# Two-expert tiles first, early masked adds, one select for two heads, and a new order of the end stage

## The chip, the cores and the metric

The kernel runs on one core of one Trainium2 chip. The metric is the time of one execution in microseconds on that core. A core has a matrix engine (PE, whose weight loads are listed as PEld), a vector engine (DVE), a scalar engine (ACT), a general engine (POOL) and a queue engine (SP) that here issues most DMA transfers. Each engine works through its own instructions in order and waits on semaphores for the others.

## The reference

The input is a query of 2048 rows by 512 columns (`T`, `E`), in float32. After a layer norm two things are computed from the same rows and added to the input:

```
xn = layernorm(x)
q1, q2, k1, k2, v = projections of xn, 16 heads, rotary on q and k
a1, a2 = causal softmax attention of (q1, k1) and (q2, k2) over v
f = rfft(a1) - lambda * rfft(a2), along the rows, times a fixed low pass
attn = rms norm(irfft(f)) @ Wout
ffn = sum over the 2 best of 8 experts of  w * (silu(xn @ w1) * (xn @ w3)) @ w2
      + (silu(xn @ sw1) * (xn @ sw3)) @ sw2
out = x + attn + ffn
```

An expert has an inner width of 352, the shared expert (`sw`) one of 704.

## The kernel before

**The stages.** Up to about 255 us of the profile the kernel does the layer norm, the gate, the projections and the first tiles of the shared expert. Then comes `middle`, up to about 1241 us: the attention, with the experts' work laid between its pieces. `ending` closes the program: the low pass, the RMS norm, the product with `Wout`, and the sum of all parts.

**The attention stream.** `middle` cuts the attention into 32 chunks, one for each pair of heads `g` (8) and each block of 512 queries `qc` (4, the last block first). A chunk is a list of units. For a unit, `scores` makes up to two products of queries and keys in PSUM (L822), ACT takes their exponential into `pt` (L835), and where the keys lie on the diagonal ("masked" units) POOL zeroes what lies above it with `affine_select` (L840). Later `values` multiplies `pt` with the values `vd` (L862), and `added` sums it on DVE for the softmax's denominator (L876 for a chunk's first, L879). When a chunk has ended, `sums` and `finish` turn its outputs and sums on PE (L888, L900, L901), DVE takes the reciprocal `rcp` (L903) and the normalised `o_n` (L908), and `put` writes it to `vd`. When all four chunks of a pair of heads are through, `folded` prepares their rows for the low pass in eight steps on POOL (on DVE for the last pair, L966 being one of its last lines). A masked unit comes in three kinds: the whole diagonal tile `d`; tiles `d+1` and `d+3` together; and tile `d+2` of both heads together (`last` in `units`).

**The loop.** The 544 units go by fours, 136 iterations of some 7 us. In each one the scores of two units come first, then the values of the units before, then the other two scores. On DVE follow the adds of units held back, the unmasked ones of the first two units, the experts' steps with the other unmasked adds between them, and at last all masked adds of the four units:

```
added(before)
added(u for u in units[:2] if not masked(u))
later = [u for u in units[2:] if not masked(u)]
while True:
    work()
    added(later[:1])
```

The engines keep the order in which the program issues (`manual_schedule`), so this text is the order on DVE. After the adds come the steps of `folded`: none if a unit of this iteration is masked, one if a unit of the next is, otherwise two.

**The experts.** `experts` is a generator; each `yield` gives its cost, and `work` calls it as often as keeps pace with the stream. It does the shared expert's tiles up to about 595 us and then 34 routed tiles of 128 rows (`NR`). The first 28 (`NP`) belong to one expert each. The other six hold 64 rows of one expert and 64 of another, and so need two experts' weights. `rows_of` gathers a tile's rows on POOL, `transposed` turns them (`xT`), `up_first` and `up_third` are the products `xh` and `xg` (L180) with a tanh between, `turned_back` turns the result into `uT` (L206 on PE, L208 and L209 on DVE), and `down` is the product `xy` (L216), which ACT scales (L225) and SP stores to `ys` (L228).

**The weights.** There are two places in SBUF, each with `wu` (1408 KB) and `wd` (768 KB). `fetch_up` (L146) and `fetch_down` (L149) load one place. Behind the second product of a tile, the `wu` places that it used are filled with what comes two halves later, and behind its down product the `wd` places:

```
for n in sets[j]:
    m = n + 2 - len(halves)
    es.append(routed(halves[n + 2]) if m < 0 else wex[NX + m : NX + m + 1])
    fetch_up(es[n + 2], n % 2, nc.sync)
```

A one-expert tile so uses one place, while the other is loading for the next tile. A two-expert tile uses both. Behind the last tiles the shared expert's weights are loaded (`wex[NX]`, `wex[NX + 1]`) for the last rows of it, which the end stage does (`wh`, L246; `ws`, L256 on ACT and L257 on DVE). SP also loads the queries `qS` (L739, eight transfers) and keys `kS` (L727) for coming chunks.

**The end.** `ending` first does the shared expert's last `wh` and `ws`, and the low pass: products of `vd` and `fold` with the table `conv` (L1141) and sums on DVE (L1186 to L1205). Meanwhile `fetched` loads the rows of the input into `res` and adds the shared expert's rows (`ysh`) and twice the routed rows (`ys`, indirect, L1125) by accumulating DMAs on POOL, 12 tiles ahead; `still` goes on with the rest. Then, for each of eight pairs of row tiles: `prepared` (`y` on DVE, its square on ACT), `means` and `scales` (root on ACT, L1227, Newton steps and `a`, L1234, on DVE), `across` (turn on PE, L1262, copy on ACT, L1264), `projected` (`po`, L1270) and `finished` (`res` plus `po`, L1275, and the store). `last` does the last tile in two halves (L1284 to L1287). Buffers come from the pools `tail1` and `tail`; `ws`, `diff` and `first` lie in `tail` with the rest. `stored(y, ysh[NT - 1], 0.5)` writes the last shared tile from DVE.

Of the kernel before, what the change touches and what calls it, by code (L numbers as in the profile page):

```python
# [47 lines left out]
NP = (T * TOP // HALF - NX) // 2  # L48
WUP = NE * 2 * FI
# [18 lines left out]
def block_kernel(  # L68
# [527 lines left out]
    def middle(general):  # L596


        with ExitStack() as pools:
# [29 lines left out]
            def experts():  # L629
# [7 lines left out]
                for t0 in range(EARLY, NT - 1, TQ):  # L637
# [3 lines left out]
                    for n, us in enumerate(chunks(xnT[:, :, cols], u_last)):  # L641
# [7 lines left out]
                        elif last and n == 3:  # L649
                            ps = bank([P, 2, NR], "ps_w")  # L650
                            for i in range(2):
                                nc.tensor.transpose(ps[:, i, :], who_sb[:, 0, :, i], ident[:NR, :NR])
                            nc.vector.tensor_copy(tok, ps[:, 0, :])
                            nc.vector.tensor_copy(wcol, ps[:, 1, :])
                        elif last and n == 5:


                            xr = [rows_of(0), rows_of(1)]
                            es = [routed(0)]
                            fetch_up(es[0], 0, nc.sync)  # L660
                        yield 3.45 * (t1 - t0) / TQ
                    if last:
                        es.append(routed(2))
# [13 lines left out]

                sets = [[j] if j < NP else [2 * j - NP, 2 * j - NP + 1] for j in range(NR)]
                halves = [2 * j + i for j in range(NR) for i in range(len(sets[j]))]
# [4 lines left out]
                def tile_down(j, uT):  # L684
                    return places(j, 1), uT, ys[j * P : (j + 1) * P, :], wcol[:, j : j + 1]

                for j in range(NR):
# [5 lines left out]
                    if j + 2 < NR:  # L693
                        xr.append(rows_of(j + 2))
# [93 lines left out]

            class Chunk:
# [21 lines left out]
                def scores(self, unit):  # L811
# [24 lines left out]
                    for _, kb, _, col, _ in unit:  # L836
                        if kb >= qc * TQ and not general:

                            part = pt[:, :, col : col + P]
                            nc.gpsimd.affine_select(  # L840
                                out=part, in_=part, pattern=[[0, 2], [1, P]], compare_op=ALU.is_ge, fill=0.0,
                                base=0, channel_multiplier=-1,
# [174 lines left out]
            def masked(entry):  # L1017
                _, c, unit = entry
                return any(kb >= c.qc * TQ for _, kb, *_ in unit)

# [8 lines left out]
            for i in range(0, len(stream), 4):  # L1029
# [22 lines left out]
                added(u for u in units[:2] if not masked(u))  # L1052
                later = [u for u in units[2:] if not masked(u)]
# [7 lines left out]
                added(u for u in units if masked(u))  # L1061
                if any(map(masked, units)) or not shared:
                    steps = 0
                else:
                    steps = 1 if any(map(masked, stream[i + 4 : i + 8])) else 2
# [25 lines left out]
    def ending():  # L1091
# [3 lines left out]
        with tc.tile_pool(name="tail1", bufs=1) as t1, tc.tile_pool(name="tail", bufs=2) as tp, tc.tile_pool(  # L1095
            name="tail_ps", bufs=4, space=PSUM
        ) as fps, tc.tile_pool(name="conv_ps", bufs=2, space=PSUM) as zps, tc.manual_schedule(
# [5 lines left out]
            _, _, _, _, (_, _, stored), _ = expert(tp, fps)  # L1103
            hidden, gated, times, _, result = shared_expert(tp, fps, 2)
# [47 lines left out]
            def copied(z):  # L1152
                diff = tp.tile([P, 2, E], F32, tag="diff", name="diff")
# [29 lines left out]
            first = tp.tile([P, E], F32, tag="first", name="first", bufs=1)  # L1183
# [128 lines left out]
            for n in range(NT // 2):  # L1312
# [4 lines left out]
                if n == 1:  # L1317
                    stored(y, ysh[NT - 1], 0.5)
                if n + 1 < NT // 2:
# [3 lines left out]
                if ahead is not None:  # L1323
                    finished(2 * n - 1, ahead)
                    still(2 * n - 1)
                if n + 2 < NT // 2:
                    pairs[n + 2].means()
                if n + 1 < NT // 2:
                    now, po = po, projected(after)
                    finished(2 * n, now)  # L1330
                    still(2 * n)
            finished(NT - 2, po)
# [137 lines left out]
```

## Time and profile before

| | |
|---|---|
| runs | 1361.46, 1357.98, 1360.07 us; median 1360.07 |
| profiled execution | 1360.14 us |
| its span, first to last instruction | 1358.3 us |
| mean granted clock of PE | 0.994 |
| busy: PE, DVE, ACT, POOL | 1312.6, 1005.4, 688.4, 626.3 us |
| stages, PE idle in them: 255 to 716 us | 1.3 us of 461 |
| 716 to 1183 us | 10.6 us of 467 |
| 1183 to 1241 us | 7.6 us of 58 |
| 1241 us to the end | 14.3 us of 117 |

The span is what lies between the first and the last instruction. An engine's busy time is the sum of its instructions; a wait in brackets in a timeline row is the idle time ahead of it on its own engine, with what ended it. `x8` in a row means eight instructions of one kind run together. The windows view gives, for each stretch, the busy time of PE, PEld, DVE, ACT and POOL with the number of instructions, then the granted clock of PE, the share of the DMA engines and GB/s. The waits view gives in one line the total, the number of times and the longest.

### The profile page before, as it was taken

How to read it: one execution, taken by the hardware profiler on the slowest of the kernel's cores; microseconds unless marked ns; L12 is line 12 of the kernel's file. 1: busy time of each engine (PE TensorE's matmuls, PEld its weight loads, DVE VectorE, ACT ScalarE, POOL GpSimd, SP SyncE). 2: the span in 40 equal slices, each digit the busy share in tenths (PEclk: the TensorE clock that was granted, in tenths of full speed). 3: DMA queues.
4: the chain of work that ended last, by engine and by line, in shares of the span. 5: the costliest groups of instructions: out<-in, count | busy, mean ns of one | idle time of the engine just before them, and what ended most of it. 6: DMA issues, size and time to landing. Idle time of an engine off the chain costs nothing.

```text
span 1358.3 us, 20810 instructions
## 1 busy us (share of the span) xinstructions
PE 1312.6 (97%) x7554; PEld 600.3 (44%) x7554; DVE 1005.4 (74%) x1344; ACT 688.4 (51%) x847; POOL 626.3 (46%) x671
## 2 busy tenths in 40 slices
PE   7999999999999999999999999899999999987998
PEld 3444444334443444445444444344544444443544
DVE  7049883287668778868889986778898788764785
ACT  2311110265656566676666666566676666640221
POOL 0002330012221323235968984778589469421764
PEclk9999999999999999999999999999999999998999
DMA  9406673200211122235665656555565666777997
GB/s 375 171 16 171 201 196 97 89 15 32 75 43 31 40 75 82 74 123 170 190 194 143 226 176 180 181 173 174 185 194 178 210 189 230 262 294 293 175 219 169
DMA packets 75578, 214.29 MB, mean 158 GB/s; under 512 B 12244, under 2 KB 12696, under 8 KB 69576
## 3 DMA queue, kind: packets, MB, share of 16 engines
q1 hardware_dynamic: 62744, 185.68, 41.7%
q0 software_dynamic: 11056, 22.78, 8.6%
q10 hardware_dynamic: 1664, 4.38, 0.9%
q8 instruction: 63, 1.03, 0.3%
q14 instruction: 51, 0.42, 0.1%
HBM read 169.69 MB, written 43.10 MB: 157 GB/s over the span
## 4 chain that ended last, share of the span: by engine, by line
PE 65%; DVE 6%; POOL 5%; DMA 3%; issue 1%; ACT 1%; SPq 0%; DVEq 0%; ACTq 0%; POOLq 0%
PE ps_o L862 16%; PE ps_s L822 12%; PE wh L246 8%; PE xy L216 6%; PE xg L180 5%; PE xh L180 5%; PE wy L284 4%; PE ps_sum L888 2%; DMA wu<-in_wex_dram 2%; POOL pt L840 1%; PE po L1270 1%; DMA wd<-in_wex_dram 1%; DVE sum L879 1%; PE ps_ot L900 1%; PE ps_x L165 1%
## 5 line engine op out<-in xcount | busy, mean ns | idle before, releaser
L879 DVE TENSOR_TENSOR sum<-sum,pt 128x1024 f32<-128x1024 f32 (+3 forms) x576 | 621.4, 1128 | 36.3 <-ACT pt L835 21.6
L835 ACT ACTIVATE pt<-ps_s 128x1024 f32<-128x1024 f32 x544 | 527.3, 1023 | 184.3 <-PE ps_s L822 131.0
L840 POOL TENSOR_SCALAR_AFFINE_SELECT pt<-pt 128x256 f32<-128x256 f32 x256 | 171.0, 693 | 358.7 <-ACT pt L835 357.5
L862 PE MATMUL ps_o<-pt,vd 128*32 128x512 f32 (+3 forms) x2560 | 268.0, 534 | 4.1 <-POOL pt L840 4.1
L822 PE MATMUL ps_s<-qS,kS 64*128 64x512 f32 (+3 forms) x1280 | 203.8, 406 | 2.0 <-DVEq L1335 1.6
L822 PEld LDWEIGHTS ps_s<-qS,kS 64*128 64x128 f32 x1280 | 97.1, 185 | 177.0 <-issue 95.9
L246 PE MATMUL wh<-xnT,wu 128*128 128x512 f32 (+1 forms) x352 | 150.4, 574 | 0.0
L862 PEld LDWEIGHTS ps_o<-pt,vd 128*32 128x32 f32 x2560 | 66.9, 109 | 125.8 <-issue 103.5
L545 PE MATMUL ps_x<-xnT,wqk_sb 128*128 128x512 f32 x256 | 110.5, 593 | 0.0
L498 POOL DMA_INDIRECT who<-pairs,slot x32 | 33.1, 1034 | 165.9 <-DVE pairs L495 104.9
L216 PE MATMUL xy<-wd,uT 128*128 128x512 f32 (+3 forms) x240 | 97.1, 606 | 7.7 <-DVE rcp L903 6.3
L246 PEld LDWEIGHTS wh<-xnT,wu 128*128 128x128 f32 x352 | 64.1, 190 | 72.7 <-issue 56.5
L180 PE MATMUL xh<-wu,xT 128*128 128x352 f32 (+1 forms) x320 | 90.5, 473 | 4.2 <-DMA wu<-in_wex_dram 3.3
L917 POOL TENSOR_TENSOR vd<-o_n 128x128 f32<-128x128 f32 x60 | 62.2, 1057 | 65.6 <-DVE o_n L908 65.5
L180 PE MATMUL xg<-wu,xT 128*128 128x352 f32 (+1 forms) x320 | 88.6, 468 | 0.0
L545 PEld LDWEIGHTS ps_x<-xnT,wqk_sb 128*128 128x128 f32 x256 | 48.4, 190 | 60.6 <-issue 60.6
L284 PE MATMUL wy<-wd,ws 128*128 128x512 f32 x160 | 74.8, 603 | 0.0
L257 DVE SCALAR_TENSOR_TENSOR ws<-ws,wh 128x512 f32<-128x512 f32 (+4 forms) x26 | 16.7, 644 | 73.6 <-ACT ws L256 73.6
L1125 POOL DMA_INDIRECT res<-ys,slot x32 | 54.9, 1715 | 25.3 <-DMA res<-ysh 13.5
L562 ACT CAST hi<-turned 128x1024 fp32r<-128x1024 f32 x16 | 16.7, 1045 | 93.9 <-DVE turned L560 70.9
L180 PEld LDWEIGHTS xh<-wu,xT 128*128 128x128 f32 (+1 forms) x320 | 48.0, 176 | 31.7 <-issue 6.5
L180 PEld LDWEIGHTS xg<-wu,xT 128*128 128x128 f32 (+1 forms) x320 | 46.6, 174 | 34.4 <-issue 14.8
(254 smaller groups left out, 1416.8 us busy)
## 6 DMA issues: line engine op xcount, KB each, us to landing
wu<-in_wex_dram SPq DMA_DIRECT2D x44, 1408.0 KB
wd<-in_wex_dram SPq DMA_DIRECT2D x43, 768.0 KB
kS<-parts_k SPq DMA_DIRECT2D x128, 128.0 KB
qS<-parts_q SPq DMA_DIRECT2D x256, 64.0 KB
ys<-y_sb SPq DMA_DIRECT2D x34, 256.0 KB
parts_q<-hi SPq DMA_DIRECT2D x32, 256.0 KB
parts_k<-hi SPq DMA_DIRECT2D x16, 256.0 KB
parts_k<-turned SPq DMA_DIRECT2D x16, 256.0 KB
```

The lines of the kernel that those rows point to most:

```text
L180: nc.tensor.matmul(dst[r, :], xT[:, c, r], w[:, o : o + FI], start=(c == 0), stop=(c == NE - 1), skip_group_check=True,)
L216: nc.tensor.matmul(y[r, :], uT[:m, ic, r], w[:m, ic * E : (ic + 1) * E], start=(ic == 0), stop=(ic == NF - 1), skip_group_check=True,)
L246: nc.tensor.matmul(dst, w_sb[o // WUP][0][:, o % WUP : o % WUP + P], x[:, c, :], start=(c == 0), stop=(c == NE - 1))
L284: nc.tensor.matmul(y, us[i][:, t * P : (t + 1) * P], w_sb[i // NF][1][:, i % NF * E : (i % NF + 1) * E], start=(i == 0), stop=(i == SCH - 1),)
L545: nc.tensor.matmul(ps[:, i, :], wqk_sb[st, qk][:, i, c, :], xnT[:, c, cols], start=(c == 0), stop=(c == NE - 1),)
L822: nc.tensor.matmul(to, k, queries[2 * g + h, qc][r, off : off + w], start=True, stop=not general)
L835: nc.scalar.activation(pt[:, :, used], ps[:, :, used], AF.Exp, scale=SCALE)
L840: nc.gpsimd.affine_select(out=part, in_=part, pattern=[[0, 2], [1, P]], compare_op=ALU.is_ge, fill=0.0, base=0, channel_multiplier=-1,)
L862: nc.tensor.matmul(self.o[r : r + 32, off:], vd[:, kb, v0 : v0 + 32], pt[:, s, :], start=first, stop=self.ended, skip_group_check=True,)
L879: nc.vector.tensor_add(to, to, pt)
L917: eng.tensor_add(vd[:, self.qc * TQ : (self.qc + 1) * TQ, v0 : v0 + 32], self.o_n[:, :, h, 0, :], self.o_n[:, :, h, 1, :],)
L1125: nc.gpsimd.indirect_dma_start(out=came[k], out_offset=None, in_=ys, in_offset=bass.IndirectOffsetOnAxis(ap=slot[:, step - 2, order[k] : o ...
```

## The change

The order of routed tiles becomes `ORDER`: the six two-expert tiles, then the 28 of one expert; `sets`, `halves`, `places` and `tile_down` follow it. The masked adds of an iteration's first two units are issued with the unmasked ones, ahead of the experts' steps; those of the other two stay at the end. In a `last` unit one `affine_select` over four blocks of 128 columns takes the place of two over two. Ahead of an iteration with masked units a step of `folded` is issued only if another pair of heads is ready or the last pair is in work. In the end stage the last shared tile is scaled and stored by ACT, `ws`, `diff` and `first` come from a pool of their own (`tail2`), and `finished` of the two tiles moves: one ahead of `across` and `prepared`, the other ahead of `means`.

```diff
NR = NS - 2
 NP = (T * TOP // HALF - NX) // 2
+ORDER = [*range(NP, NR), *range(NP)]
 WUP = NE * 2 * FI
 WCOL = WUP + NF * E
 CONVS = 23
...
                         elif last and n == 5:
-                            xr = [rows_of(0), rows_of(1)]
-                            es = [routed(0)]
+                            xr = [rows_of(j) for j in ORDER[:2]]
+                            es = [routed(2 * ORDER[0])]
                             fetch_up(es[0], 0, nc.sync)
                         yield 3.45 * (t1 - t0) / TQ
                     if last:
-                        es.append(routed(2))
+                        es.append(routed(2 * ORDER[0] + 1))
                         fetch_up(es[1], 1, nc.sync)
                     for t in range(t0, t1):
                         y = result(us, t - t0, range(NF))
...
                 xT, late = transposed(xr.pop(0)), None
                 yield 0.6
-                sets = [[j] if j < NP else [2 * j - NP, 2 * j - NP + 1] for j in range(NR)]
-                halves = [2 * j + i for j in range(NR) for i in range(len(sets[j]))]
+                sets, halves = [], []
+                for tj in ORDER:
+                    n = 1 if tj < NP else 2
+                    sets.append(range(len(halves), len(halves) + n))
+                    halves += [2 * tj + i for i in range(n)]
                 def places(j, part):
                     return [w_sb[n % 2][part] for n in sets[j]]
                 def tile_down(j, uT):
-                    return places(j, 1), uT, ys[j * P : (j + 1) * P, :], wcol[:, j : j + 1]
+                    tj = ORDER[j]
+                    return places(j, 1), uT, ys[tj * P : (tj + 1) * P, :], wcol[:, tj : tj + 1]
                 for j in range(NR):
                     if j > 0:
...
                     yield 2.9 if late else 2.4
                     u = up_third(places(j, 0), xT, half)
                     if j + 2 < NR:
-                        xr.append(rows_of(j + 2))
+                        xr.append(rows_of(ORDER[j + 2]))
                     for n in sets[j]:
                         m = n + 2 - len(halves)
...
                 nc.vector.tensor_copy(shift, ps.rearrange("p t q -> p (t q)"))
                 return shift
+            def masked(chunk, unit):
+                return any(kb >= chunk.qc * TQ for _, kb, *_ in unit)
             class Chunk:
...
                     pt = pp.tile([P, 2, QC], F32, tag="pt", name="pt")
                     used = slice(min(c for *_, c, _ in unit), max(c + w for *_, c, w in unit))
                     nc.scalar.activation(pt[:, :, used], ps[:, :, used], AF.Exp, scale=SCALE)
-                    for _, kb, _, col, _ in unit:
-                        if kb >= qc * TQ and not general:
-                            part = pt[:, :, col : col + P]
+                    if masked(self, unit) and not general:
+                        cols = [col for *_, col, _ in unit]
+                        if cols == [0, 2 * P]:
+                            chosen = [pt.rearrange("p s (h q) -> p (s h) q", h=2)[:, :, :P]]
+                        else:
+                            chosen = [pt[:, :, col : col + P] for col in cols]
+                        for part in chosen:
                             nc.gpsimd.affine_select(
-                                out=part, in_=part, pattern=[[0, 2], [1, P]], compare_op=ALU.is_ge, fill=0.0,
-                                base=0, channel_multiplier=-1,
+                                out=part, in_=part, pattern=[[0, part.shape[1]], [1, P]], compare_op=ALU.is_ge,
+                                fill=0.0, base=0, channel_multiplier=-1,
                             )
                     ready = []
                     for h, kb, off, col, w in unit:
...
                 nonlocal worked
                 worked += next(ex, work_all)
-            def masked(entry):
-                _, c, unit = entry
-                return any(kb >= c.qc * TQ for _, kb, *_ in unit)
             def added(entries):
                 for n, c, unit in entries:
...
                     c.finish()
                 held, before = [], held
                 added(before)
-                added(u for u in units[:2] if not masked(u))
-                later = [u for u in units[2:] if not masked(u)]
+                added(units[:2])
+                later = [u for u in units[2:] if not masked(*u[1:])]
                 while True:
                     work()
                     added(later[:1])
...
                     if worked / (work_all - left) >= (i + 4) / len(stream):
                         break
                 added(later)
-                added(u for u in units if masked(u))
-                if any(map(masked, units)) or not shared:
+                added(u for u in units[2:] if masked(*u[1:]))
+                if any(masked(*u[1:]) for u in units) or not shared:
                     steps = 0
+                elif any(masked(*u[1:]) for u in stream[i + 4 : i + 8]):
+                    steps = 1 if ready or units[0][1].g == NG - 1 else 0
                 else:
-                    steps = 1 if any(map(masked, stream[i + 4 : i + 8])) else 2
+                    steps = 2
                 for _ in range(steps):
                     if folding is None and ready:
                         folding = folded(ready.pop(0), nc.gpsimd)
...
-        with tc.tile_pool(name="tail1", bufs=1) as t1, tc.tile_pool(name="tail", bufs=2) as tp, tc.tile_pool(
-            name="tail_ps", bufs=4, space=PSUM
-        ) as fps, tc.tile_pool(name="conv_ps", bufs=2, space=PSUM) as zps, tc.manual_schedule(
+        with tc.tile_pool(name="tail1", bufs=1) as t1, tc.tile_pool(name="tail2", bufs=2) as t2, tc.tile_pool(
+            name="tail", bufs=2
+        ) as tp, tc.tile_pool(name="tail_ps", bufs=4, space=PSUM) as fps, tc.tile_pool(
+            name="conv_ps", bufs=2, space=PSUM
+        ) as zps, tc.manual_schedule(
             engines={mybir.EngineType.PE, mybir.EngineType.DVE, mybir.EngineType.Activation, mybir.EngineType.Pool}
         ):
             conv = t1.tile([P, CONVS * P], F32, name="conv")
             nc.scalar.dma_start(conv[:, : 11 * P], conv_t[:, : 11 * P])
             nc.scalar.dma_start(conv[:, 11 * P :], conv_t[:, 11 * P :])
-            _, _, _, _, (_, _, stored), _ = expert(tp, fps)
-            hidden, gated, times, _, result = shared_expert(tp, fps, 2)
+            _, _, _, _, (_, _, stored), _ = expert(tp, fps, by_scalar=True)
+            hidden, gated, times, _, result = shared_expert(t2, fps, 2)
             fetch_down(wex[NX + 1 : NX + 2], 1, nc.scalar)
             wo_sb = t1.tile([P, NE, E], F32, name="wo_sb")
             nc.scalar.dma_start(wo_sb, wout.rearrange("(c p) e -> p c e", p=P))
...
                 return z
             def copied(z):
-                diff = tp.tile([P, 2, E], F32, tag="diff", name="diff")
+                diff = t2.tile([P, 2, E], F32, tag="diff", name="diff")
                 nc.scalar.copy(diff, z)
                 return diff
...
             zr = pair("ps_r")
             product(zr[:, 0, :], [(0, vd[:, 0, :])])
             product(zr[:, 1, :], [(1, vd[:, 1, :])])
-            first = tp.tile([P, E], F32, tag="first", name="first", bufs=1)
+            first = t2.tile([P, E], F32, tag="first", name="first", bufs=1)
             nc.scalar.copy(first, zr[:, 1, :])
             z4 = at(0, fold, 2)
             nc.vector.tensor_add(low[:, 0], zr[:, 0, :], first)
...
                     pairs[n + 1].scales()
                 if n == 1:
                     stored(y, ysh[NT - 1], 0.5)
+                if ahead is not None:
+                    finished(2 * n - 1, ahead)
+                    still(2 * n - 1)
                 if n + 1 < NT // 2:
                     aT = across(2 * n + 2)
                 if n + 2 < NT // 2:
                     pairs.append(prepared(n + 2))
-                if ahead is not None:
-                    finished(2 * n - 1, ahead)
-                    still(2 * n - 1)
-                if n + 2 < NT // 2:
-                    pairs[n + 2].means()
                 if n + 1 < NT // 2:
                     now, po = po, projected(after)
                     finished(2 * n, now)
                     still(2 * n)
+                if n + 2 < NT // 2:
+                    pairs[n + 2].means()
             finished(NT - 2, po)
             last(NT - 1, after)
```

## The prediction

> **What bounds the kernel now.** I read part 1 of the page first, then the waits of TensorE, then the timelines round the longest of them, and last the end of the program.
>
> ```profile
> PE 1312.6 (97%) x7554; PEld 600.3 (44%) x7554; DVE 1005.4 (74%) x1344; ACT 688.4 (51%) x847; POOL 626.3 (46%) x671
> ```
> TensorE is busy for 1312.6 of 1358.3 us. No matmul is added or taken away, so an edit can only win idle time of PE (some 46 us in all) and matmuls that run long. The profiled execution took 1360.14 us, 1.84 us over its span; the median of the runs is 1360.07, so both are one base. A difference below 0.3%, 4.1 us, I count as none: a measurement cannot tell it.
>
> The waits of PE from 255 to 1160 us (total, times, longest):
> ```profile
> PE xy L216 <- DVE rcp L903: 6.3, 4, 3.3
> PE ps_o L862 <- POOL pt L840: 4.1, 4, 1.6
> ```
> Four times an expert's down product waits for a reciprocal on VectorE, and four times a value product for a masked `pt`. The DVE timeline at the first large one (start, us, operation):
> ```profile
> 821.03 0.52 DVE L191 SCALAR_TENSOR_TENSOR xtanh<-xtanh,xh 128x352 f32<-128x352 f32 x1 [1.90 <-ACT xtanh L190]
> 824.76 0.53 DVE L197 TENSOR_TENSOR xtanh<-xg,xtanh 128x352 f32<-128x352 f32 x1 [3.21 <-PE xg L180]
> 825.20 5.48 DVE L879 TENSOR_TENSOR sum<-sum,pt 128x1024 f32<-128x1024 f32 x7
> 830.61 0.25 DVE L903 RECIPROCAL rcp<-ps_st 128x16 f32<-128x16 f32 x1
> ```
> DVE idles 3.21 us for an expert's product, and only then does seven adds; the reciprocal comes behind them, and PE stops 1.43 us.
>
> The PE timeline at the end of the middle stage, where the two-expert tiles lie:
> ```profile
> 1195.28 4.27 PE L180 MATMUL xh<-wu,xT 128*64 128x352 f32 x14 [2.67 <-DMA wu<-in_wex_dram]
> 1216.87 2.58 PE L180 MATMUL xh<-wu,xT 128*64 128x352 f32 x14 [0.68 <-DMA wu<-in_wex_dram]
> 1230.42 5.26 PE L246 MATMUL wh<-kept,wu 128*128 128x128 f32 x32 [2.34 <-DMA wu<-in_wex_dram]
> 1236.39 1.04 PE L216 MATMUL xy<-wd,uT 128*64 128x512 f32 x2 [0.70 <-DVE vd L966]
> 1238.16 2.79 PE L216 MATMUL xy<-wd,uT 128*64 128x512 f32 x10 [0.73 <-DMA wd<-in_wex_dram]
> ```
> Five waits for weights, 7.1 us (the fourth is put down to DVE, but `uT` was there at 1228.7: a weight load is likelier). The same stretches in the windows view (PEclk is the number before the DMA share):
> ```profile
> 1195.28:1199.55 4.27, 4.27 (x16) 1.58 (x16) 0.27 (x2) 0.00 (x0) 0.00 (x0) 0.60 0.58 242
> 1230.42:1235.68 5.26, 5.26 (x32) 5.07 (x32) 4.92 (x23) 0.00 (x0) 0.00 (x0) 0.71 0.99 410
> ```
> Behind idles of 2.67 and 2.34 us the clock fell. The first group took 4.27 us where the same 14 matmuls took 2.58 after the 0.68 us idle: 1.7 us more. The second is 5.26 x 0.71 = 3.7 us at full clock: 1.5 more.
>
> **Part 1, the order of tiles.** Removed at the tail: 2.67 + 1.7 + 0.68 + 2.34 + 1.5 + 0.70 + 0.73 = 10.3 us. One-expert tiles fetch a tile ahead into the other weight place, so I take all of it (bounds 6 to 10.3: single fetches already pass unseen in the middle, but the DMA engines are near full here). A second fetch of the same 768 KB down weights is added at the end; its rate is 410 GB/s by the row above, 1.9 us of transfer, behind everything that is waited for there.
>
> Added in front: the pair of loads (2.88 MB) is issued when the second product of one tile ends and needed at the first product of the next. SP's and PE's timelines:
> ```profile
> 609.36 0.35 SPq L146 DMA_DIRECT2D wu<-in_wex_dram  x1
> 616.15 2.63 PE L180 MATMUL xh<-wu,xT 128*128 128x352 f32 x8 [0.73 <-ACT xT L167]
> 1183.28 1.55 SPq L146 DMA_DIRECT2D wu<-in_wex_dram  x2
> ```
> The room in front is 6.8 us for the second tile (609.36 to 616.15), then 9.7, 9.6, 6.6 and 10.3; the first one-expert tile needs one load after 5.0. The pair at the tail landed at most 9.1 to 10.4 us after its issue where nobody waited, and 12.0 where PE did (1183.28 to 1195.28). I take 10.0: 3.2 us at the second tile and 3.4 at the fifth, each with 1.7 us of slow clock, nothing at three others, and 6.2 - 5.0 = 1.2 for the single load (6.2 from the issue at 1224.18 to 1230.42): 11.2 us. Low bound 9.1 us without slow clock: 2.3 + 2.5 = 4.8. High bound 12.0 us everywhere: 5.2 + 2.3 + 2.4 + 5.4 + 1.7 + 3 + two clock losses 3.4 = 23.4, since eight q loads are issued at 610.09 right behind the pair. Queued behind the pair on SP are only q, k and down-weight loads with a unit or more of room. Net: +0.9 us (-5.5 to +13).
>
> The Trainium skill (TensorE: Matmul & The Clock Gate, "What's actually happening") puts the fall of the clock after an idle window of about 3.4 us, free-running. The trace disagrees in size: 2.34 us of idle was enough for 0.71. By the page, none of these idles need cost clock; 3.2 us would leave both sides, and the net would stay near +1.
>
> **Part 2, the adds.** The masked adds of an iteration's first two units go ahead of the experts' DVE work. At 821.6 to 824.8, and in the same way at 842.8 (2.84 us idle) and 1063.7 (3.21), the idle takes about three of the queued adds (5.48 / 7 = 0.78 us each), and the reciprocal comes 2 to 3 us sooner. Idles before `xy` were 0.20, 1.43, 3.27 and 1.35 us, and the group after 3.27 took 4.54 instead of 2.74: 8.1 us in all. Taken: 7.0, for a remainder of the 3.27; bounds 2 and 8. What queues behind the new place is the experts' tanh product, and PE's transposition of it; the adds now wait there for the selects. At 1058.5 to 1061.8 six selects were done before the idle that takes the adds, so this wait is hidden there. Where POOL is late (selects from 753.14 on) the product would come about 5 us later, yet PE wants it only at 765.6.
>
> What the adds cost their neighbours, from POOL's timeline:
> ```profile
> 753.14 5.07 POOL L840 TENSOR_SCALAR_AFFINE_SELECT pt<-pt 128x256 f32<-128x256 f32 x6
> 822.06 0.77 POOL L840 TENSOR_SCALAR_AFFINE_SELECT pt<-pt 128x256 f32<-128x256 f32 x2 [2.49 <-ACT pt L835]
> ```
> A select takes 0.39 us where DVE idles and 0.85 where it adds. More selects will now meet adds: some already do (all eight at 878.02, 6.68 us, meet them), so I charge nothing and keep the price for a rival. A rule of the Trainium skill speaks against this part: SBUF — State Buffer, "Who interferes with whom", says that a VectorE operation with two SBUF inputs and a GpSimd one that reads SBUF lock each other out entirely, the later one waiting to the end. The row has the mean select doubled, not stopped for a whole 0.78 us add each time; by the rule each would take up to 1.2 us, and the rival below would be dearer by four fifths.
>
> **Part 3, selects and folds.** One select over 4 x 128 replaces two in 32 units. The work is the same; what is saved is at most the fixed part of 0.39 us, on POOL, which delays PE in only four places: -0.3 us (0 to -1). The four fold steps on POOL that move out of the iteration ahead of masked units are not those ahead of the stalls at 757.72, 882.60 and 1119.11: 0 us, cover being POOL's idle of several us there (0.5 us each if it is gone).
>
> **Part 4, the end stage.** ScalarE and PE (start, us):
> ```profile
> 1247.12 0.38 ACT L256 ACTIVATE ws<-wh 128x256 f32<-128x256 f32 x1 [5.39 <-DMA ys<-y_sb]
> 1249.75 15.67 PE L1141 MATMUL ps_z<-xnT,conv 128*128 128x512 f32 x32 [2.55 <-DVE vd L1187]
> ```
> `ws` shares its buffer's history with the stored tile, and so waits for a store; DVE waits for `ws`, PE for DVE. In a pool of its own `ws` is free: 2.55 us, and the 1.3 us by which those 32 matmuls run long (14.4 at full clock). But the end has a second chain: the same store, then loads of `res` and 32 indirect accumulates on POOL at some 3 us each.
> ```profile
> 1345.97 1.54 POOL L1125 DMA_INDIRECT res<-ys,slot  x1 [2.00 <-DMA res<-ys,slot]
> 1351.43 0.42 DVE L1286 TENSOR_TENSOR res<-res,po 128x256 f32<-128x256 f32 x1 [1.04 <-PE po L1284]
> ```
> The last accumulate is issued at 1345.97 and used at 1351.43; the shortest landing of its kind is 5.0 us, so it has under 0.5 us to spare. PE would run ahead and wait for it. The store of the last `y`, moved to ScalarE, frees 0.68 us of DVE at 1299, and `finished` moves ahead of a wait for the mean; these shift no more than the same half microsecond. Taken: -1.0 us (0 to -3.8).
>
> **Sum.** 1360.1 + 0.9 - 7.0 - 0.3 - 1.0 = 1352.7 us.
>
> **Rivals.** (a) *The front covers the pairs*: loads land in 9.1 us and the clock holds; net of part 1 is 4.8 - 10.3 = -5.5, so 1346.3. For it: pairs at 1146.03 and 1165.24 were not waited for. Against: 6.8 us of room is below any landing seen. (b) *The end passes its gain on*, because accumulates start earlier too: -3.8 instead of -1.0, 1349.9. Against it stands the half microsecond above. (c) *The reciprocals stay late*, since the moved adds wait for selects that meet adds: 0 instead of -7, 1359.7. For it: DVE already idled 2.59 us for a select at 878.46. (d) *The front is the dearer end*: 12.0 us landings all through, 23.4 - 10.3 = +13.1, 1364.9; it outweighs the rest once the front's waits pass 18.6 us. (e) *Selects beside adds hold up the value products*, the main case on the slower side. In about 16 iterations PE's load of `pt` follows the select with no slack (0.25 to 0.37 us of wait); two selects each 0.44 us longer cost 16 x 0.88 = 14 us: 1366.7. It outweighs the gain of 7.4 us if more than 8 of these places are hit.
>
> **How the numbers follow.** Main case 0.44, (a) 0.11, (b) 0.12, (c) 0.12, (d) 0.09, (e) 0.12. Faster by over 0.3% (below 1356.0) is main without its upper edge, 0.39, with (a) and (b): 0.62. Within 0.3%: (c), 0.05 of main, and the near halves of (d) and (e): 0.22. Slower: 0.16. The range 1345 to 1365 leaves out most of (e), half of (d) and the lowest of (a).
>
> **What would show it.** Right: no wait of `xy` on `rcp` over 0.5 us, no wait on `wu` past 1180 us, two new ones of 3 to 4 us between 610 and 680, `ws` starting within 1 us of `wh`, and the last `res` waiting for its accumulate. Wrong: `ps_o` waiting for POOL by more than 8 us in all, front waits beyond 17 us, or a store landing between `xy`'s end and the accumulates later than before.

## The result, and the profile after

The changed kernel takes 1382.01 us (median of 4 runs, 1379.65 to 1383.05) against 1360.76 us before: a ratio of 1.0158, 95% interval 1.0137 to 1.0178. It is 21 us slower, where 8 us less had been forecast, and the time lies outside the range of 1345 to 1365 us. The profiled execution took 1379.65 us, the least of the four; its span is 1377.9 us, 19.6 more than before, and it is these 19.6 us that the stages below add up to.

The waits of PE over the whole span of the changed kernel, as far as they bear on the forecast (us in total, times, longest):

```profile
PE xh L182 <- DMA wu<-in_wex_dram: 35.4, 5, 11.8
PE ps_tr L1275 <- DVE a L1247: 5.1, 3, 2.8
PE ps_o L875 <- POOL pt L853: 2.5, 3, 1.4
PE xy L218 <- DVE rcp L916: 1.2, 1, 1.2
PE ps_z L1154 <- DVE vd L1200: 1.0, 1, 1.0
```

The wait on the reciprocal went from 6.3 to 1.2 us, nearly as forecast (none over 0.5 us); the wait of `xh` for up weights, 3.3 before, is 35.4. All five pieces of it lie in front, in the PE timeline of the changed kernel:

```profile
621.51 1.41 PE L182 MATMUL xh<-wu,xT 128*64 128x352 f32 x2 [5.78 <-DMA wu<-in_wex_dram]
627.25 4.96 PE L182 MATMUL xh<-wu,xT 128*64 128x352 f32 x14 [4.34 <-DMA wu<-in_wex_dram]
695.19 1.40 PE L182 MATMUL xh<-wu,xT 128*64 128x352 f32 x2 [11.63 <-DMA wu<-in_wex_dram]
698.46 3.96 PE L182 MATMUL xh<-wu,xT 128*64 128x352 f32 x14 [1.87 <-DMA wu<-in_wex_dram]
747.49 5.03 PE L182 MATMUL xh<-wu,xT 128*128 128x352 f32 x8 [11.76 <-DMA wu<-in_wex_dram]
```

They stand where the prediction put them: at the second and the fifth two-expert tile and at the first one-expert tile. Only they are far longer, and the matmuls behind them run slow (14 of them take 4.96 and 3.96 us, where 2.58 us is the time behind a short wait in the kernel before).

The loss can be followed stage by stage. The exponentials of the attention (`pt` on ACT, 544 in both kernels) start 0.4 us later than before at 593 us, 13.7 later after the first stop, 31.1 after the second and 46.2 after the third. From there the lag falls to 37.3 us at iteration 132 of 136. The last expert product `xy` ends 20.8 us later than before (1261.7 against 1240.95), the span 19.6 later. So the front lost 46 us, the middle won 9, the tail 16.5 and the end stage 1.2. At the tail PE waits for nothing any more:

```profile
1251.94 2.63 PE L182 MATMUL xg<-wu,xT 128*128 128x352 f32 x8
1255.19 2.84 PE L218 MATMUL xy<-wd,uT 128*128 128x512 f32 x6
1258.88 2.84 PE L218 MATMUL xy<-wd,uT 128*128 128x512 f32 x6
1261.57 2.17 PE L248 MATMUL wh<-kept,wu 128*128 128x128 f32 x18
```

The last row is work that before stood ahead of the last `xy`: 2.2 of the tail's 16.5 us are only moved into the end stage, which has thus won 3.4 of its own.

What was slow in front is in SP's timeline of the changed kernel, and in the windows of it (PE, PEld, DVE, ACT, POOL busy, then the granted clock, the DMA share and GB/s):

```profile
675.30 2.25 SPq L733 DMA_DIRECT2D kS<-parts_k  x4
678.91 1.54 SPq L148 DMA_DIRECT2D wu<-in_wex_dram  x2
```

```profile
605.50:609.50 4.00, 4.00 (x36) 1.65 (x24) 4.00 (x6) 3.25 (x4) 4.00 (x6) 1.00 0.13 50
629.90:639.50 9.60, 9.60 (x83) 4.18 (x79) 4.77 (x7) 4.61 (x6) 0.71 (x1) 0.84 0.14 51
687.70:701.20 13.50, 4.14 (x12) 1.52 (x14) 0.00 (x0) 0.00 (x0) 0.00 (x0) 0.50 0.64 227
```

The pair of up weights was issued behind the k loads, 2.4 us after the second product had ended (676.5), and PE got the first place 16.3 us after the issue (695.19) and the second 19.6 us after it (698.46). The first two windows lie behind the issues of four k loads (603.03 and 627.57): the engines are 0.13 to 0.14 busy, that is two of sixteen, and move 50 GB/s. Four k loads are 0.5 MB, which at that rate takes 10.5 us. A pair that is issued meanwhile seems to have its share on these two engines too, and to end there long after the rest. The trace records sixteen completions for each load of weights, and they say so: of those of the pair's first place fourteen came 7.6 to 8.8 us after the issue, and the last two 15.5 and 16.1 us after it. The third window shows the price on PE: clock 0.50 for 13.5 us, which begin inside the stop.

The other pairs show the same by contrast. The three that were issued 1.9 to 5.0 us after a chunk's last k load (609.67, 678.91 and 731.16) stopped PE. The three that came over 10 us after one (639.88, 658.32 and 709.77) had landed 9.3 to 10.3 us after their issue, and nothing waited.

The page of before had that row already, at the same place, and I did not read it:

```profile
604.00:609.00 5.00, 5.00 (x36) 2.44 (x32) 3.79 (x4) 4.40 (x6) 5.00 (x8) 1.00 0.13 50
```

It had the landings too, which the completions give: the single loads of up weights that were issued 1.8 to 5.2 us after a last k load (609.36, 626.09, 662.18 and 698.94) landed after 12.6, 14.1, 16.1 and 17.1 us, and the two between them without one (644.12 and 678.53) after 6.5 and 7.3 us. There PE had no need of them yet.

### The profile page after: what moved, and what is told of

Its sections match the earlier page's. It is cut to its first block, busy times and chain, and to the rows that moved or that the text cites. A ratio compares the mean times of both kernels' runs of the same rounds, so it can differ in the third digit from the quotient of the medians.

```text
span 1377.9 us, 20779 instructions
## 1 busy us (share of the span) xinstructions
PE 1313.0 (95%) x7554; PEld 600.7 (44%) x7554; DVE 1014.5 (74%) x1343; ACT 689.0 (50%) x848; POOL 627.8 (46%) x639
## 4 chain that ended last, share of the span: by engine, by line
PE 64%; DMA 6%; POOL 5%; DVE 3%; issue 1%; SPq 1%; ACT 1%; ACTq 0%; DVEq 0%; POOLq 0%
PE ps_o L875 16%; PE ps_s L831 12%; PE wh L248 8%; PE xy L218 6%; PE xh L182 6%; PE xg L182 5%; PE wy L286 4%; DMA wu<-in_wex_dram 4%; PE po L1283 2%; PE ps_sum L901 2%; POOL pt L853 1%; DMA wd<-in_wex_dram 1%; PE ps_ot L913 1%; PE ps_x L167 1%; PE ps_u L208 1%
## 5 line engine op out<-in xcount | busy, mean ns | idle before, releaser
L892 DVE TENSOR_TENSOR sum<-sum,pt 128x1024 f32<-128x1024 f32 (+2 forms) x576 | 630.7, 1143 | 30.5 <-POOL pt L853 14.1
L853 POOL TENSOR_SCALAR_AFFINE_SELECT pt<-pt 128x256 f32<-128x256 f32 (+1 forms) x224 | 165.0, 759 | 387.2 <-ACT pt L844 347.6
L182 PE MATMUL xh<-wu,xT 128*128 128x352 f32 (+1 forms) x320 | 95.9, 500 | 35.5 <-DMA wu<-in_wex_dram 35.4
L930 POOL TENSOR_TENSOR vd<-o_n 128x128 f32<-128x128 f32 x60 | 59.0, 1002 | 67.6 <-DVE o_n L921 67.6
L193 DVE SCALAR_TENSOR_TENSOR xtanh<-xtanh,xh 128x352 f32<-128x352 f32 x34 | 17.4, 513 | 69.7 <-ACT xtanh L192 69.7
L564 ACT CAST hi<-turned 128x1024 fp32r<-128x1024 f32 x16 | 16.7, 1046 | 93.8 <-DVE turned L562 59.2
L192 ACT ACTIVATE xtanh<-xh 128x352 f32<-128x352 f32 x34 | 15.8, 464 | 94.3 <-PE xh L182 94.3
```

What stands on the lines that cost most here:

```text
L182: nc.tensor.matmul(dst[r, :], xT[:, c, r], w[:, o : o + FI], start=(c == 0), stop=(c == NE - 1), skip_group_check=True,)
L853: nc.gpsimd.affine_select(out=part, in_=part, pattern=[[0, part.shape[1]], [1, P]], compare_op=ALU.is_ge, fill=0.0, base=0, channel_multip ...
L892: nc.vector.tensor_add(to, to, pt)
L930: eng.tensor_add(vd[:, self.qc * TQ : (self.qc + 1) * TQ, v0 : v0 + 32], self.o_n[:, :, h, 0, :], self.o_n[:, :, h, 1, :],)
```

## The experiments

Times are medians, and ratios are to the kernel before, run on the same chip beside them. The edits are shown in short; `...` stands for lines left out.

**The parts by themselves.** First the order of tiles alone:

```diff
+ORDER = [*range(NP, NR), *range(NP)]
-sets = [[j] if j < NP else [2 * j - NP, 2 * j - NP + 1] for j in range(NR)]
+for tj in ORDER:
...
```

> Only the order of the routed tiles is changed. If the order alone pays (46 us lost to weight waits of PE up to 750 us, 16 us won after 1178 us of before's time), this takes 1360 + 46 - 16 = 1390 us, with five waits of xh on wu of some 35 us in all. If the other parts have a share in the long waits in front (POOL or DVE later, so fetches issued later), the waits are under 25 us and the time lies below 1380 us.

1390.88 us, 1.0239 (1.0221 to 1.0258). The waits of PE from 600 to 800 us:

```profile
PE xh L182 <- DMA wu<-in_wex_dram: 36.8, 5, 12.6
```

The order alone makes the whole loss, and has no helper.

Then everything else, without the order:

```diff
+added(units[:2])
+steps = 1 if ready or units[0][1].g == NG - 1 else 0
+chosen = [pt.rearrange("p s (h q) -> p (s h) q", h=2)[:, :, :P]]
...
+_, _, _, _, (_, _, stored), _ = expert(tp, fps, by_scalar=True)
+hidden, gated, times, _, result = shared_expert(t2, fps, 2)
...
```

> All of the change but the order of tiles. If the parts are independent, this keeps the 9 us that the changed kernel won between 770 and 1216 us and some 1 to 2 us of the end stage: 1349 to 1352 us, with the wait of xy on rcp near 1 us and the tail's weight waits of before. If the win in the middle is a gift of PE's stops in front, which let DVE and POOL catch up, it takes 1356 to 1360 us.

1350.42 us, 0.9936 (0.9920 to 0.9952). The gains of the middle and of the end do not hang on the stops in front. The two results add up: +31.2 - 9.3 = +21.9 against +21.3 measured.

The masked adds alone:

```diff
-added(u for u in units[:2] if not masked(u))
+added(units[:2])
-added(u for u in units if masked(u))
+added(u for u in units[2:] if masked(u))
```

> Only the masked adds of the first two units are moved ahead. By the prediction's term: 7 us less, 1353 us, xy waiting on rcp 1 us instead of 6.3, waits of ps_o on POOL about as before (4 us). By the rival of selects beside adds: ps_o waits on POOL for 8 us or more and the time is 1360 us or above.

1353.56 us against 1359.7, 0.9962 (0.9945 to 0.9979): 6.1 us less. The waits of PE from 255 to 1160 us:

```profile
PE ps_o L862 <- POOL pt L840: 3.0, 5, 1.4
PE xy L216 <- DVE rcp L903: 1.0, 1, 1.0
```

The reciprocal's 6.3 us are down to 1.0, and the rival (selects beside adds) is refuted: `ps_o` waits less on POOL than before, not more. The selects did get slower, a median of 586 ns instead of 407, and the adds waited longer for them (DVE 28.7 us in all instead of 10.2), but PE did not feel it. The prediction's price of a select beside adds was too low all the same: its 0.85 us is a mean of six, two of which had started before the adds. One by one, in the kernel before:

```profile
753.50 0.41 POOL L840 TENSOR_SCALAR_AFFINE_SELECT pt<-pt 128x256 f32<-128x256 f32 x1
753.68 1.29 DVE L879 TENSOR_TENSOR sum<-sum,pt 128x1024 f32<-128x1024 f32 x1
753.86 1.39 POOL L840 TENSOR_SCALAR_AFFINE_SELECT pt<-pt 128x256 f32<-128x256 f32 x1
```

That they contend at all agrees with the Trainium skill (SBUF — State Buffer, "Who interferes with whom"). The 1.39 us are also nearer to the 1.2 us that the prediction worked out by that rule than to its own 0.85.

The end stage alone:

```diff
-_, _, _, _, (_, _, stored), _ = expert(tp, fps)
-hidden, gated, times, _, result = shared_expert(tp, fps, 2)
+_, _, _, _, (_, _, stored), _ = expert(tp, fps, by_scalar=True)
+hidden, gated, times, _, result = shared_expert(t2, fps, 2)
...
```

> Only the end stage is changed (pool of its own for ws, diff and first, the last shared tile by ACT, the order of finished). If the accumulating DMAs hold the end, as the prediction had it: 0 to 1 us less. If they follow PE: 2 to 4 us less, and the last accumulate lands over 2 us ahead of its use.

1356.54 us, 0.9972 (0.9960 to 0.9984): 3.2 us less. DVE's timeline at the end:

```profile
1347.28 0.69 DVE L1277 TENSOR_TENSOR res<-res,po 128x512 f32<-128x512 f32 x1 [4.18 <-DMA res<-ys,slot]
1349.61 0.75 DVE L1288 TENSOR_TENSOR res<-res,po 128x256 f32<-128x256 f32 x2 [1.64 <-DMA res<-ys,slot]
```

Both expectations have a share. The accumulating DMAs hold the end: DVE waits 4.18 and 1.64 us for them, as the prediction had it. But they hold it later than the term allowed: the last accumulate is issued at 1344.69 (1345.97 before) and used at 1349.61 for both halves of the last tile. Before, the halves were added at 1351.43 and 1353.15, and the slack had been measured at the first of them, though the second ends the program.

The end stage also has a cost that the prediction left out. PE's waits for `a` were 2.7 us in three pieces before. Here they are

```profile
PE ps_tr L1264 <- DVE a L1236: 5.7, 4, 2.8
```

and in the changed kernel 5.1 us. The same edit puts `means`, from which `a` is made, behind `finished`; whether that is the reason was not tried.

The select and the fold steps alone:

```diff
+cols = [col for *_, col, _ in unit]
+if cols == [0, 2 * P]:
+    chosen = [pt.rearrange("p s (h q) -> p (s h) q", h=2)[:, :, :P]]
...
+elif any(map(masked, stream[i + 4 : i + 8])):
+    steps = 1 if ready or units[0][1].g == NG - 1 else 0
```

> Only the one select for two heads and the moved fold steps. By the prediction's term 0.3 us less (0 to 1). If POOL, freed a little ahead of the late selects at 755 us, also shortens waits of ps_o on POOL: 1 to 2 us less.

1363.35 us, 1.0026 (1.0016 to 1.0036): 3.6 us more, which neither expectation has. PE from 740 to 1200 us:

```profile
PE xy L216 <- DVE rcp L907: 7.4, 4, 3.7
PE ps_o L866 <- POOL pt L844: 4.6, 5, 1.6
```

The two old waits are 1.8 us longer (6.1 and 4.1 before, in the same stretch). And one stretch of half clock is new, behind a stop of 1.58 us at 756.22:

```profile
756.30:759.60 3.30, 3.30 (x18) 1.39 (x19) 3.20 (x4) 0.63 (x1) 3.13 (x3) 0.50 0.58 214
```

It costs 1.7 us. The kernel before has the same stop of 1.58 us at 757.72 with no slow clock behind it. In that stretch of the stream (iterations 69 to 132) the exponentials fall back by 5.3 us, so some 2 us are not placed. Which of the two edits does it was not tried. With the adds in front no cost is seen: 1359.7 - 6.1 - 3.2 = 1350.4 us for adds and end stage alone, and 1350.42 for all three.

**What makes the pair land late.** Three runs take traffic out of the changed kernel or reshape it. The first leaves out q and k loads:

```diff
 def load_keys(g, c):
...
+        if (g, c) == (3, 0) or g == 4:
+            keys[h, c] = keys[h - 2, c]
+            continue
...
 def load_queries(g, qc):
...
+        if g == 3 or (g, qc) == (4, NQC - 1):
+            queries[h, qc] = queries[4 + h % 2, 0]
+            continue
```

> The changed kernel without the q loads of five chunks and the k loads of one pair of heads that lie between 600 and 770 us (these chunks compute with the q and k already there). If a pair of up weights lands late because those loads share the DMA engines with it: each of them is 1 MB less to move, at some 250 to 300 GB/s, so the five waits on wu fall from 35.4 us to about 15 to 20, and 20 us or more are won with the slow clock behind them. If the pair's own 2.9 MB and its issue set the landing: over 30 us of waits stay.

1353.27 us (one run); the waits of PE from 600 to 800 us:

```profile
PE xh L182 <- DMA wu<-in_wex_dram: 6.6, 3, 3.2
```

Even less than expected: the q and k loads are nearly all of the 35.4 us. The second leaves out down weights:

```diff
-for n in sets[j - 1]:
+for n in sets[j - 1] if j > 6 else ():
     fetch_down(es[n + 2], n % 2, nc.sync)
```

> The changed kernel without the fetches of down weights behind the first six down products (the tiles compute with the down weights already there). If the down weights, issued 3 to 4 us behind the up weights, take half of the engines from them: the waits at the fifth two-expert tile and at the first one-expert tile fall by 4 to 6 us each, those at the second tile stay (no down weights are under way there), 35.4 becomes about 25. If transfers are served in order of issue, the waits on wu stay as they are, but for the pair issued behind older down weights (2 to 4 us).

1380.57 us (one run); the same view:

```profile
PE xh L182 <- DMA wu<-in_wex_dram: 35.4, 5, 12.1
```

Nothing changes, to the tenth. Up to 9 MB (12 loads of 768 KB) less to move brings nothing, while some 5 MB of q and k bring 29 us. So it is not the sum of the bytes; but the down weights are issued behind the pair and the k loads ahead of it, so place in the queue could still be the reason. The third keeps all bytes, and only cuts each k load in two. A k load reads 32 rows of `parts_k` twice, through a leading dimension of 2 with step zero:

```diff
-nc.sync.dma_start(
-    k[64 * s : 64 * s + 64, :].bitcast(F32), src.unsqueeze(0).to_broadcast([2, 2 * D, QC]))
+for b in range(2):
+    r = 64 * s + 32 * b
+    nc.sync.dma_start(k[r : r + 32, :].bitcast(F32), src)
```

> The changed kernel with each k load (64 rows of 2 KB, a source read twice) cut into two plain loads of 32 rows, like the q loads; the bytes stay. During k loads the trace has some 24 packets of 2 KB in a us, two engines' worth, for 11 us, and a pair of up weights issued meanwhile ends on two engines long after the other fourteen. If the form of the k loads keeps them on two engines: the waits on wu fall from 35 us to 10 to 15, the time to 1355 to 1362 us. If it is the bytes or the 2 KB packets of q and k alike: 30 us or more stay, and the time is 1380 us.

1354.48 us, 0.9956 (0.9940 to 0.9972): 28 us below the changed kernel, with the same tiles in the same order. The waits of PE from 255 to 1160 us, and the window behind the k loads, issued here from 603.35 on:

```profile
PE xh L182 <- DMA wu<-in_wex_dram: 12.1, 4, 3.6
```

```profile
603.40:609.50 6.10, 6.10 (x50) 2.55 (x46) 6.10 (x7) 4.82 (x6) 6.10 (x7) 1.00 0.37 98
```

The share is 0.37 where it was 0.13, the loads are through before the pair comes, and 12.1 us of waits are left. The sixteen completions of the fifth tile's first place now come together, 5.4 to 5.9 us after its issue. The form of the k load is the cause of the late landing. The Trainium skill says why: DMA: Bandwidth & Descriptors, "Rules for kernel authors", has it that the outermost dimension of a transfer's access pattern decides over how many engines it is spread, and that a leading broadcast of c copies confines it to at most c engines, the lowest-numbered ones according to "Why a DMA increments its semaphore by 16 and not by 1". The rows agree in number, since 0.13 of 16 is 2.1 engines; which two they are no run here shows.

Part of the 12.1 us that are left has another cause than the landing: the pair is issued late. At the fifth tile, in PE's and SP's timelines of this run:

```profile
667.20 2.59 PE L182 MATMUL xg<-wu,xT 128*64 128x352 f32 x16
661.13 7.62 SPq L744 DMA_DIRECT2D qS<-parts_q  x8
668.79 3.83 SPq L735 DMA_DIRECT2D kS<-parts_k  x8
673.46 1.54 SPq L148 DMA_DIRECT2D wu<-in_wex_dram  x2
```

The second product ended at 669.79, and SP was among its q and k issues for 3.7 us more. At the first one-expert tile it is 2.9 us (714.20 to 717.10).

**Other places for the two-expert tiles.**

```diff
-ORDER = [*range(NP, NR), *range(NP)]
+ORDER = [*range(3), 28, *range(3, 8), 29, *range(8, 13), 30, *range(13, 18), 31, *range(18, 23), 32, *range(23, 27), 33, 27]
...
```

> The changed kernel with the two-expert tiles spread out, one behind every four or five one-expert tiles, the last tile being a one-expert tile. Then only one place has to come in the short room: if waits come from two places in one room (2.9 MB in 6 to 10 us), the front keeps at most 1 to 2 us for each of the six tiles and the tail's 16 us are won: 1340 us. If every tile next to a pair meets the other loads (1.4 MB landing in over 10 us), 12 rooms cost 2 us each: 1358 us or more.

1417.39 us, 1.0423 (1.0401 to 1.0445). PE from 255 to 1290 us:

```profile
PE xh L183 <- DMA wu<-in_wex_dram: 34.6, 5, 15.7
PE xy L219 <- DMA wd<-in_wex_dram: 17.6, 3, 7.6
```

The second expectation has the sign, at far more than its price: single stops reach 15.7 us. Tight rooms spread over the whole stream meet k loads all along it: the loads for which PE waited at 679.69, 820.34 and 1042.62 (10.1, 7.6 and 15.7 us) were issued 1.6 to 2.0 us after a chunk's last k load, and of their sixteen completions the last two came 14.4 to 16.7 us after the issue, the others within 10.5. This order was not run with the k loads cut.

```diff
-ORDER = [*range(NP, NR), *range(NP)]
+ORDER = [*range(NP - 2), *range(NP, NR), NP - 2, NP - 1]
...
```

> The changed kernel with the two-expert tiles ahead of the last two one-expert tiles. The weights of the end are then fetched early, as with the tile order of the change: 5 to 10 us won against the variant without the order (1350 us). The six tiles are done some 20 us earlier, where q and k loads still run: if these make the landing late, two or three waits of 4 to 8 us eat it and the time is 1350 us or above.

1346.5 us, 0.9895 (0.9872 to 0.9918). PE from 255 to 1230 us still has

```profile
PE xh L183 <- DMA wu<-in_wex_dram: 9.1, 4, 3.4
```

It beats both kernels. With the k loads cut as well:

> The two-expert tiles ahead of the last two one-expert tiles, and the k loads cut into loads of 32 rows. If k loads on two engines cause the waits left there (9.1 us at 1075, 1100 and 1162): these fall under 3 us, the time from 1346.5 to about 1339 us. If SP, with eight issues more per chunk, holds up the weights' issue: 1347 us or above.

1337.62 us, 0.9838 (0.9822 to 0.9854), the fastest of all; 1.1 us is left of that wait. SP's four more issues per chunk (eight k loads for four) cost nothing that shows in this order. And the cut alone, in the old order, with the rest of the change:

> All of the change but the order of tiles, with the k loads cut into loads of 32 rows. No pair of loads meets k loads in the old order but the ones behind 1146 us, so 1350 us stays within 3 us if k loads matter only through pairs; 3 us or more less if they also hold up the pairs of the tail.

1350.24 us, 0.9934 (0.9914 to 0.9954), as without the cut (1350.42): in the old order the k loads cost nothing, since the weight loads behind them have room.

## Why the prediction was wrong

**Part 1, the step that failed.** The front was priced at 11.2 us (4.8 to 23.4) and cost 46. The term that was mis-sized is the landing of a pair: 10.0 us, at most 12.0, taken from rows behind 1146 us. SP issues its last k load at 1086.5, so those rows are from a stretch without k loads. In front, behind k loads, PE got the first place 11.8 to 16.3 us after the issue and both of them 17.6 and 19.6 us after it; away from k loads 10.0 was right (9.3 to 10.3). I named q loads as the neighbour and put them at 12.0; by the runs it is the k loads, on two engines. With the k loads cut, the exponentials are 22.2 us late behind the third stop instead of 46.2: the form of the k loads makes 24 us of the loss. Of the other 22, 11 were priced.

A second step failed in the same place. The pair was taken to be issued when the second product ends, but SP was still busy with q and k issues at the fifth tile and at the first one-expert tile, for 2.4 and 2.6 us in the changed kernel. From the issue to the stop the fifth tile had 4.7 us of room (678.91 to 683.56), where 6.6 had been read.

Rival (d), the dear front, had the right place and sign, and half of the price; 0.09 was too little for it, since its high end was a row from the quieter stretch.

**The clock.** 3.4 us were charged for two stops, by rows behind stops of 2.67 and 2.34 us. It became three stops, with more slow work behind each:

```profile
619.50:632.90 13.40, 7.06 (x20) 2.50 (x20) 0.16 (x1) 0.46 (x1) 0.00 (x0) 0.50 0.45 136
738.90:752.40 13.50, 4.91 (x8) 2.52 (x8) 0.00 (x0) 0.00 (x0) 0.00 (x0) 0.50 0.76 270
```

With the window from 687.70 shown above, PE was busy for 16.1 us in three stretches of clock 0.50 (13.4 to 13.5 us of each), which is 8 us lost. That this clock falls to half agrees with the Trainium skill (TensorE: Matmul & The Clock Gate, "What's actually happening"); its idle of about 3.4 us before that does not agree with the 2.34 of before. In the clock records of all fourteen profiled executions the changes lie on a grid of 3.41 us. Past the first 30 us the clock fell 56 times, each time behind a piece of that grid in which PE was busy for 54% or less, and it fell behind no fuller one; between 45 and 54% it did either. So where a stop falls on the grid decides whether it costs clock, as the two stops of 1.58 us show (PE was busy for 45% of the one piece and for 54% of the other). With 35.4 us of waits, less 0.7 that stood there before, this makes 43 of the 46 us; 3 I did not place.

**The tail.** 10.3 us priced, 16.5 measured, 14.3 without the `wh` that moved. Of the 4.0 us above the term, 2.4 are small slow pieces that I had not counted: the first two `xh` of both last pairs (0.81 us each instead of 0.32), an idle of 0.41 at 1220.56 and the `xy` at 1236.39 and 1238.16 (3.83 us instead of 2.80). The rest I did not place.

**Part 2** was right in mechanism and size: 7.0 priced, 6.1 measured alone, the wait gone where it was forecast. **Part 3**: -0.3 priced, +3.6 alone, nothing seen in company; why it costs anything alone is only in part placed. **Part 4**: -1.0 priced, -3.2 alone; the second chain is there, and the failed step is its slack, taken against the first half's add (1351.43) and not the second's (1353.15). In the changed kernel the chain is also shorter (1274.23 to 1363.41, 89.2 us, against 93.4), and PE ends the program; why it is shorter stays open. So the sign named for this part failed as well, for the last `res` waits for PE and not for its accumulate:

```profile
1371.00 0.42 DVE L1299 TENSOR_TENSOR res<-res,po 128x256 f32<-128x256 f32 x1 [1.04 <-PE po L1297]
```

**Sum.** Without part 1 the forecast would have been 1351.8 us, and 1350.42 was measured. That is partly luck: part 2 gave 0.9 us less than priced and part 4 2.2 more. The 1354.48 us with the k loads cut are near the forecast by luck too, since front (22 us for 11.2) and tail (16.5 for 10.3) were both priced too low. With part 1, the sum rested on a balance of two terms of 10 us that were both taken from the same stretch of the trace.

## What to carry to other kernels

A landing time belongs to the traffic in which it was seen: before work is moved to another place, read there which transfers run and, in the windows view, the DMA share beside the GB/s, since a low share with a transfer under way can mean few engines and not a free queue (here 0.13 at 50 GB/s). Read also when the queue engine gets to the issue, and not only when the program allows it. A prefetch with room to spare hides a transfer that sits on two engines; the same transfer sets the time once a load of all engines has to land within 7 us. Look at the outermost dimension of small loads before moving large ones: cutting the broadcast k load in two was worth 28 us in the changed order, 9 us with the two-expert tiles late, and nothing in the old one.

## What the runs showed of the hardware

- A load with a leading broadcast of 2 ran on two of the sixteen DMA engines (share 0.13, 50 GB/s); the same bytes as plain loads of 32 rows had a share of 0.37 (98 GB/s).
- A weight load issued 2 us behind such loads had fourteen of its sixteen completions after 7.6 to 8.8 us and the last two after 15.5 and 16.1; behind plain k loads all sixteen came after 5.4 to 5.9. Leaving out other weight loads issued after it changed no wait (35.4 us both times).
- The clock of PE was 0.50 for 13.5 us round stops of 5.8 + 4.3, 11.6 + 1.9 and 11.8 us, beginning 3.1 to 4.1 us into them; in the kernel before, stops of 2.3 and 2.7 us cost 1.5 and 1.7 us. Over all profiled executions, past their first 30 us, it fell only behind pieces of a 3.41 us grid in which PE was busy for 54% or less.
- A masked select on POOL took 0.41 us alone and up to 1.39 beside an add on DVE. With the adds moved beside them the median of all selects grew from 407 to 586 ns; DVE waited 28.7 us for them instead of 10.2, PE 3.0 instead of 4.1.
